# Two graph layers on one core: GpSimd sums Wh's rows for the mean, six blocks of adj come late, Wh runs seven blocks ahead

## The chip, the cores and the metric

The kernel runs on one core of a Trainium2 chip. The metric is the device time of one execution in microseconds; lower is better. Each core has five engines with instruction queues of their own: TensorE (PE in the profile; its weight loads are PEld), VectorE (DVE), ScalarE (ACT), GpSimd (POOL) and SyncE (SP, which here only issues DMAs). DMAs are also issued from the queues of ACT and GpSimd.

## What is computed

x is 4096 x 512 in float32. adj is 4096 x 4096 in int32, with about four ones in a row. Two layers follow one another:

```
Wh   = einsum(x, W)                        # 8 heads of 64
f1, f2 = Wh . a[:, :64], Wh . a[:, 64:]    # a number per node and head
e    = leaky_relu(f1[:, None] + f2[None, :], 0.2), and -9e15 where adj is 0
x1   = layernorm(x + softmax(e) @ Wh)

agg  = (mask @ x1) / max(deg, 1)
out  = layernorm(x1 + relu(concat(x1 @ W_self + b_self, agg @ W_nb + b_nb) @ W_comb + b_comb))
```

A row of adj without a single one gives a softmax over equal values: the node gets the mean of all rows of Wh. That mean is what a part of this change is about.

## The kernel before

The nodes are cut into 32 blocks of 128 (P). The kernel turns each row of adj into a list of its neighbours, and then gathers rows by index from tables in DRAM, with no dense product over adj. The order of the instructions of each engine is the order in which the program text issues them (`manual_schedule`); each engine works through its own in that order, with semaphores between engines.

**First stage** (the loop at L979, `for b in range(LB)`). For each block b of adj, SP loads two halves of 1 MB (`load_adj`, buffers `at`, four of them), two blocks ahead. ACT turns a half into bfloat16 and counts it (`mask_adj`, L448, three `ab` buffers). TensorE folds a block's masks into keys (`fold_adj`, L467), and VectorE takes the eight largest of each quarter (`max_keys`, L482). Every fourth block, `decode` turns four blocks' keys into neighbour lists, indices (`idx`) and owner masks (`own`). It is a generator with 16 stops; `some(lists)` runs it from stop to stop, in this loop four times a step. Near its end it builds four step tiles on VectorE (`place(b)`, L545 and L546), which TensorE multiplies (L551).

Beside that, Wh is computed block by block (w). `transposed` turns x's block on TensorE and ACT copies it out as xT; `node_half` multiplies xT with the weights, 264 columns at a time (L376), and VectorE copies the result to `row` (L380). GpSimd copies three small parts (`node_rest`) and stores the row to table t0 (`store`, L976). There are 32 node blocks and 27 loop steps, so the steps in AHEAD = (1, 6, 11, 16, 20) do two node blocks. The last row is stored by SP, after the loop (L1010).

For the mean, `transposed` also sums x over the nodes: for most blocks with four ACT copies that carry a sum (L368), for four of them with a reduction on VectorE (L365), and for the last three with additional transposes (`only=True`). `mean_row` then multiplies the mean of x by the weights at steps 23 to 26 and stores it as row 1 of t0. Row 0 of t0 is a pad whose scores are very negative; node n is in row n + 2.

**Late blocks.** Blocks LB + 1 to 31 of adj (28 to 31) are not loaded in this loop. After it, `load_late` brings quarters of 0.5 MB, and `mask_late` (L967, ACT) masks them; the dictionary MASKS says how many at each step of the attention loop. A block whose four quarters are in is folded and maximised at the next step (`full`).

**The crossing** (L1010 to L1058). SP stores the last row, loads two late quarters and the weights w_nb and w_comb, which TensorE multiplies together (`fold_weights`, L302 and L314; `place` takes `row` buffers). GpSimd gathers the first blocks from t0, five rows for each node (`gather`, L641: k = 0 is the node's first neighbour, k = 1 to 4 are shared slots). Blocks LB - 1 and LB are folded here. The decode of blocks 24 to 27 starts here (L1033), with its step tiles in a `row` buffer (`on_row`), and runs on at the first attention steps.

**The attention loop** (L1066, i from -3). A step works on several blocks at once: a_shared(i+1) on TensorE (L715), gathers for block i+6 once a buffer is free, a_weights and a_weigh on VectorE (L672, L690), a_first (L698) on VectorE and a_own_sum (L708) on ACT, the layer norm on ACT, the transposition (L355) and a_z (L759). At i == TURN (8) the lists of blocks 28 to 31 begin to be decoded, and w_self is loaded into m1, which up to then holds the late quarters. The third stage does the second layer in the same manner, from table t1.

Of the kernel before, what the change touches and what calls it, by code (L numbers as in the profile page):

```python
# [40 lines left out]
P = 128  # L41
# [72 lines left out]
def listed_layers(  # L114
# [33 lines left out]
    AHEAD = (1, 6, 11, 16, 20)  # L148
    EARLY = NB - 3
    LB = NB - 5  # L150
    FIRST = (0, 1, 3, *range(LB + 1, NB))

    t0 = tc.dram_tile([N + 2, FW], F32, name="t0")
    t1 = tc.dram_tile([N + 2, HD], F32, name="t1")
# [120 lines left out]
    def pads(wp):  # L275
        pad = wp.tile([P, FW], F32, name="row", bufs=3)
        nc.vector.memset(pad[0:1, 0:H], -BIG)
        nc.vector.memset(pad[0:1, H:FW], 0.0)
        nc.scalar.dma_start(t0[0:1, :], pad[0:1, :])
        nc.scalar.dma_start(t1[0:1, :], pad[0:1, H:TW])  # L280
        nc.scalar.dma_start(t1[1:2, :], pad[0:1, H:TW])
# [67 lines left out]
    def transposed(b, wp, sums=None, only=False):  # L349

        tp = ps.tile(
            [P, FB, P], F32, name="pw" if only else "tp", bufs=2 if only else 1
        )
        for c in range(FB):
            nc.tensor.transpose(tp[:, c, :], xs[:, b, ts(c, P)], ident)  # L355
        if only:
            t = tp
        else:
            t = wp.tile([P, FB, P], F32, name="xT", bufs=4)
        if sums is None or b >= EARLY and not only:  # L360
            nc.scalar.copy(t, tp)
        elif only or b % 2 == 0 and b < XL:
            if not only:
                nc.scalar.copy(t, tp)
            nc.vector.tensor_reduce(sums[:, :, b : b + 1], tp, AX.X, OP.add)  # L365
        else:
            for c in range(FB):
                nc.scalar.activation(  # L368
                    t[:, c, :], tp[:, c, :], AF.Copy, accum_out=sums[:, c, b : b + 1]
                )  # L370
        return t
# [10 lines left out]
    def node_first(b, xT, w_sb, row, between):  # L382
# [5 lines left out]
        for n, (k, r) in enumerate(parts):  # L388
# [6 lines left out]
            if n == 2:  # L395
                fold_adj(between, dp)
                max_keys(between)
            if n > 1:
# [9 lines left out]
    def mean_row(w_sb, sums, xa):  # L408

        xm = small.tile([P, FB], F32, name="xm", bufs=1)  # L410
        nc.vector.tensor_reduce(xm, sums, AX.X, OP.add)
        nc.vector.tensor_scalar(xm, xm, 1.0 / N, None, OP.mult)
        yield
        mr = xa.tile([1, FW], F32, name="mr")
        mf = small.tile([1, H], F32, name="mf", bufs=1)
        for k in range(2):
            pq = ps.tile([1, HW], F32, name="sm", bufs=2)
            for c in range(FB):
                nc.tensor.matmul(
                    pq, lhsT=xm[:, c : c + 1], rhs=w_sb[:, c, k * HW : (k + 1) * HW],  # L420
                    start=(c == 0), stop=(c == FB - 1),
                )
            nc.vector.tensor_copy(
                mr[0:1, k * HH : (k + 1) * HH], pq[:, (1 - k) * H : (1 - k) * H + HH]
            )
            if k == 0:
                nc.vector.tensor_copy(mf, pq[:, 0:H])
                yield
        nc.gpsimd.dma_start(t0[1:2, 0:H], mf)
        nc.gpsimd.dma_start(t0[1:2, TW:FW], mf)  # L430
        nc.gpsimd.dma_start(t0[1:2, H:TW], mr[0:1, 0:HD])
        yield
# [51 lines left out]
    def decode(b0, dp, place):  # L484
# [36 lines left out]
        nc.vector.tensor_scalar(L[:, :, 0:1], L[:, :, 0:1], 1.0, None, OP.max)  # L521
        nc.vector.tensor_scalar(idx[:, bs, 0:K0], L[:, :, 0:K0], float(N + 1), None, OP.min)
# [127 lines left out]
    def gather(table, b, g, at=None):  # L650
        for k in range(KS) if table is t0 else (*range(1, KS), 0):
# [970 lines left out]
```

## Time and profile before

| | us |
|---|---|
| median of three runs | 659.75 (653.55 to 661.48) |
| the profiled execution's own time | 768.31 |
| its span, first to last instruction | 766.6 |
| busy: PE, DVE, ACT, POOL | 596.7, 410.3, 408.9, 356.4 |
| last `row` copy of the first stage ends | 201.3 |
| first gather from t0 starts | 204.33 |

All times in what follows are of that one profiled execution, measured from its first instruction. In lists of groups, a line reads: source line, engine, operation, output <- inputs, shapes, how many | busy time and mean ns of one | idle time of the engine before them and what ended it. In timelines, a line has the start, the length, the engine, the line, the operation, and in brackets how long the engine stood idle before and who released it. "remote" and "issue" mean that the profile names no releaser. An x of 8 for matmuls stands for four float32 matmuls, recorded as two passes each.

### The profile page before, as it was taken

What the parts mean: (1) busy time and instruction counts of PE and PEld (TensorE: products, weight loads), DVE (VectorE), ACT (ScalarE), POOL (GpSimd) and SP (SyncE); (2) the same over time, 40 slices, a digit from 0 to 9 for tenths busy, and PEclk for the clock granted to TensorE, in tenths of its full rate; (3) what the DMA queues carried; (4) which work ended last, traced back from release to release, by engine and by line L of the source; (5) the groups of instructions that cost most, each with busy time, mean ns of one, the idle gap of its engine ahead of it and who ended that gap; (6) DMA issues with size and microseconds to landing.
All of it is one profiled execution on the core that took longest, in us unless ns stands there. A gap on an engine that the chain in (4) does not pass through costs nothing.

```text
span 766.6 us, 9427 instructions
## 1 busy us (share of the span) xinstructions
PE 596.7 (78%) x2582; PEld 296.2 (39%) x2582; DVE 410.3 (54%) x1186; ACT 408.9 (53%) x1066; POOL 356.4 (46%) x475
## 2 busy tenths in 40 slices
PE   6798898989763677797596678875956997877794
PEld 4576576766431232343242333332312332222231
DVE  6265869768773566566666655564212423333243
ACT  3588887887511376664454446453324434443355
POOL 4112111221475355654565544465566666666630
PEclk9799999999867798988898898998988899999998
DMA  8999999999795599886876756677678787777762
GB/s 267 408 407 409 408 409 407 410 386 389 267 327 145 166 309 323 302 270 215 255 210 209 241 175 201 222 225 240 232 215 269 238 273 254 242 248 242 256 223 86
DMA packets 92197, 210.44 MB, mean 275 GB/s; under 512 B 13854, under 2 KB 13862, under 8 KB 92138
## 3 DMA queue, kind: packets, MB, share of 16 engines
q1 hardware_dynamic: 63296, 114.32, 40.5%
q0 software_dynamic: 28656, 95.18, 39.8%
q8 instruction: 23, 0.38, 0.2%
q10 hardware_dynamic: 186, 0.28, 0.2%
q14 instruction: 36, 0.29, 0.1%
HBM read 175.91 MB, written 33.82 MB: 274 GB/s over the span
## 4 chain that ended last, share of the span: by engine, by line
PE 36%; issue 15%; DMA 14%; DVE 11%; another core or an unknown queue 11%; ACT 11%; SPq 1%; POOL 0%; DVEq 0%; ACTq 0%; POOLq 0%
DMA at<-in_adj_dram 12%; PE pw L759 6%; PE pw L376 6%; PE pw L785 5%; PE nm L785 5%; PE num L715 4%; ACT ab L448 3%; PE pw L314 3%; PE nm L792 2%; PE pw L792 2%; DVE g L690 1%; DVE sm L808 1%; PE tp L355 1%; DVE num L728 1%
## 5 line engine op out<-in xcount | busy, mean ns | idle before, releaser
L641 POOL DMA_INDIRECT g<-t,idx x290 | 276.3, 953 | 193.0 <-issue 85.5
L759 PE MATMUL pw<-wr,xT 128*128 128x512 f32 x256 | 130.1, 655 | 8.1 <-issue 8.1
L376 PE MATMUL pw<-w_sb,xT 128*128 128x264 f32 x496 | 125.8, 400 | 2.9 <-DVE row L380 1.4
L448 ACT ACTIVATE ab<-at 128x2048 bf16<-128x2048 int32 x56 | 107.1, 1916 | 33.2 <-DMA at<-in_adj_dram 27.0
L376 PEld LDWEIGHTS pw<-w_sb,xT 128*128 128x128 f32 x496 | 91.9, 194 | 28.1 <-issue 3.4
L715 PE MATMUL num<-g,own 128*32 128x256 f32 (+1 forms) x512 | 40.6, 441 | 54.7 <-ACT num L708 50.0
L759 PEld LDWEIGHTS pw<-wr,xT 128*128 128x128 f32 x256 | 50.8, 209 | 75.9 <-issue 73.5
L402 POOL COPY lst<-row 128x8 f32<-128x8 f32 x32 | 6.9, 216 | 151.9 <-DVE row L380 121.7
L690 DVE TENSOR_TENSOR g<-g,ew 128x2048 f32<-128x2048 f32 x32 | 73.1, 2283 | 2.1 <-ACT xs L754 1.3
L785 PE MATMUL nm<-m,xT 128*128 128x512 f32 x128 | 62.5, 627 | 6.8 <-issue 5.4
L785 PE MATMUL pw<-m,xT 128*128 128x512 f32 x128 | 64.5, 643 | 3.6 <-issue 2.0
L723 DVE RECIPROCAL rd<-num 128x8 f32<-128x8 f32 x32 | 6.6, 208 | 104.6 <-PE num L715 46.9
L808 DVE SCALAR_TENSOR_TENSOR sm<-g,lst,nm 128x512 f32<-128x512 f32 x15 | 11.3, 754 | 82.5 <-remote 45.1
L355 PE MATMUL tp<-ident,xs 128*128 128x128 f32 x256 | 41.5, 287 | 14.0 <-ACT xT L368 6.8
L776 ACT COPY nm<-brow 128x512 f32<-128x512 f32 x16 | 9.4, 585 | 76.5 <-DVE sm L808 45.2
L355 PEld LDWEIGHTS tp<-ident,xs 128*128 128x128 f32 x256 | 31.9, 147 | 38.0 <-issue 24.2
L680 ACT ACTIVATE ew<-e 128x40 f32<-128x40 f32 x32 | 6.6, 206 | 74.8 <-issue 35.5
L380 DVE COPY row<-pw 128x264 f32<-128x264 f32 x62 | 26.4, 426 | 31.9 <-PE pw L376 24.5
L763 ACT COPY row<-pw 128x512 f32<-128x512 f32 x32 | 18.7, 584 | 46.0 <-remote 23.6
L715 PEld LDWEIGHTS num<-g,own 128*32 128x32 f32 x512 | 14.5, 119 | 73.4 <-ACT num L708 56.5
L785 PEld LDWEIGHTS pw<-m,xT 128*128 128x128 f32 x128 | 25.3, 205 | 43.8 <-issue 39.0
L785 PEld LDWEIGHTS nm<-m,xT 128*128 128x128 f32 x128 | 24.1, 197 | 44.5 <-issue 38.2
(240 smaller groups left out, 967.1 us busy)
## 6 DMA issues: line engine op xcount, KB each, us to landing
at<-in_adj_dram SPq DMA_DIRECT2D x56, 1024.0 KB
m<-in_adj_dram SPq DMA_DIRECT2D x16, 512.0 KB
xt<-xT SPq DMA_DIRECT2D x32, 256.0 KB
t<-row SPq DMA_DIRECT2D x32, 256.0 KB
xT<-xt SPq DMA_DIRECT2D x32, 256.0 KB
out_dram<-row SPq DMA_DIRECT2D x32, 256.0 KB
t<-row POOLq DMA_DIRECT2D x31, 264.0 KB
xs<-in_x_dram SPq DMA_DIRECT2D x31, 256.0 KB
```

The lines of the kernel that those rows point to most:

```text
L314: nc.tensor.matmul(mp, lhsT=wT[:, d, :], rhs=wc[:, d, :], start=(d == 0), stop=(d == FB - 1))
L355: nc.tensor.transpose(tp[:, c, :], xs[:, b, ts(c, P)], ident)
L376: nc.tensor.matmul(pw, lhsT=xT[:, c, :], rhs=w_sb[:, c, k * HW : (k + 1) * HW], start=(c == 0), stop=(c == FB - 1),)
L380: nc.vector.tensor_copy(row[:, k * HW : (k + 1) * HW], pw)
L448: nc.scalar.activation(ab, loads.pop((b, h)), AF.Relu, accum_out=asum[:, b, h : h + 1])
L641: nc.gpsimd.indirect_dma_start(out=out, out_offset=None, in_=table, in_offset=bass.IndirectOffsetOnAxis(ap=at, axis=0),)
L690: nc.vector.tensor_tensor(gv, gv, E[b][:, sl].unsqueeze(3).to_broadcast([P, sl.stop - sl.start, H, D]), OP.mult,)
L715: nc.tensor.matmul(NM[b][ts(k, HP), a * HD : a * HD + r.stop - r.start], lhsT=OWN[b][:, k, :], rhs=G0[b][:, K0 + k, r], start=False, stop= ...
L759: nc.tensor.matmul(pz, lhsT=xT[:, c, :], rhs=m2[:, c, :], start=(c == 0), stop=(c == FB - 1))
L785: nc.tensor.matmul(NM[b], lhsT=xT[:, c, :], rhs=m1[:, c, :], start=False, stop=(c == FB - 1), skip_group_check=True,)
L792: nc.tensor.matmul(NM[b][ts(k, HP), :], lhsT=OWN[b][:, k, :], rhs=g[:, K0 + k, 0:HD], start=False, stop=True, tile_position=(0, k * HP), s ...
L808: nc.vector.scalar_tensor_tensor(yp, Y[b], lst[:, b, KL + 1 : KL + 2], NM[b], OP.mult, OP.add)
```

## The change

1. LB goes from 27 to 25: blocks 26 to 31 of adj come late, six instead of four, and the loop has 25 steps. AHEAD becomes seven steps, (0, 3, 6, 9, 12, 16, 20).
2. The sums over x are gone. GpSimd adds each row of Wh, but the last, into `acc` (`add_row`), after the row's store. `mean_row` multiplies `acc` and the last row by a column of 1/4096 on TensorE, and SP stores the result as row N + 2 of t0. It stands after the last row's store and after block 24's fold, ahead of the late loads.
3. Row 1 of t0 becomes a second pad. In `decode`, a node without neighbours gets index N + 2 for k = 0. In `gather`, the own row (k = 0) comes last for both tables, and the others read a view of t0 without its last row.
4. In a doubled step, the second transposition and the second mask of the next block are issued between the two halves of the first node block (`then`).
5. The decode of blocks 24 to 27 no longer starts in the crossing. It starts in the attention loop, at the step where block 27's maxima are taken (i = 2), and its step tiles lie in an xT buffer. MASKS now runs to i = 11, so TURN is 12; w_self's fold moves from steps 10, 15, 20, 25 to 15, 19, 23, 27.

```diff
-    AHEAD = (1, 6, 11, 16, 20)
-    EARLY = NB - 3
-    LB = NB - 5
+    AHEAD = (0, 3, 6, 9, 12, 16, 20)
+    LB = NB - 7
...
-        nc.scalar.dma_start(t0[0:1, :], pad[0:1, :])
-        nc.scalar.dma_start(t1[0:1, :], pad[0:1, H:TW])
-        nc.scalar.dma_start(t1[1:2, :], pad[0:1, H:TW])
+        for r in range(2):
+            nc.scalar.dma_start(t0[r : r + 1, :], pad[0:1, :])
+            nc.scalar.dma_start(t1[r : r + 1, :], pad[0:1, H:TW])
+        nc.scalar.dma_start(t1[N + 2 : N + 3, :], pad[0:1, H:TW])
...
-        if sums is None or b >= EARLY and not only:
-            nc.scalar.copy(t, tp)
-        elif only or b % 2 == 0 and b < XL:
-            if not only:
-                nc.scalar.copy(t, tp)
-            nc.vector.tensor_reduce(sums[:, :, b : b + 1], tp, AX.X, OP.add)
-        else:
-            for c in range(FB):
-                nc.scalar.activation(
-                    t[:, c, :], tp[:, c, :], AF.Copy, accum_out=sums[:, c, b : b + 1]
-                )
+        t = wp.tile([P, FB, P], F32, name="xT", bufs=4)
+        nc.scalar.copy(t, tp)
...
+    def add_row(b, row):
+        if b == 0:
+            nc.gpsimd.tensor_copy(acc, row)
+        else:
+            nc.gpsimd.tensor_tensor(acc, acc, row, OP.add)
+
+    def mean_row(row, wp):
+
+        mr = wp.tile([P, FW], F32, name="row", bufs=3)
         for k in range(2):
+            r = slice(k * HW, (k + 1) * HW)
             pq = ps.tile([1, HW], F32, name="sm", bufs=2)
-            for c in range(FB):
-                nc.tensor.matmul(
-                    pq, lhsT=xm[:, c : c + 1], rhs=w_sb[:, c, k * HW : (k + 1) * HW],
-                    start=(c == 0), stop=(c == FB - 1),
-                )
...
-        nc.gpsimd.dma_start(t0[1:2, 0:H], mf)
-        nc.gpsimd.dma_start(t0[1:2, TW:FW], mf)
-        nc.gpsimd.dma_start(t0[1:2, H:TW], mr[0:1, 0:HD])
-        yield
+            for n, t in enumerate((acc, row)):
+                nc.tensor.matmul(pq, lhsT=inv_n, rhs=t[:, r], start=(n == 0), stop=(n == 1))
+            nc.vector.tensor_copy(mr[0:1, r], pq)
+        nc.sync.dma_start(t0[N + 2 : N + 3, :], mr[0:1, :])
...
-        nc.vector.tensor_scalar(L[:, :, 0:1], L[:, :, 0:1], 1.0, None, OP.max)
-        nc.vector.tensor_scalar(idx[:, bs, 0:K0], L[:, :, 0:K0], float(N + 1), None, OP.min)
+        ni = dp.tile([P, G, K0], F32, name="ni", bufs=1)
+        nc.vector.tensor_scalar(ni, L[:, :, 0:K0], 0.0, float(N + 2), OP.is_equal, OP.mult)
+        nc.vector.scalar_tensor_tensor(
+            idx[:, bs, 0:K0], L[:, :, 0:K0], float(N + 1), ni, OP.min, OP.max
+        )
...
-        for k in range(KS) if table is t0 else (*range(1, KS), 0):
+        for k in (*range(1, KS), 0):
             rows_of(
-                g[:, k, 0 : table.shape[1]], table, (idx if at is None else at)[:, b, k : k + 1]
+                g[:, k, 0 : table.shape[1]], table if k == 0 or at is not None else table[0 : N + 2, :],
+                (idx if at is None else at)[:, b, k : k + 1],
             )
...
         if not keep:
             store(w, row, nc.gpsimd)
+            add_row(w, row)
...
-    def on_row(b):
+    def on_xT(b):
         if b % G == 0:
-            steps_at[0] = wp.tile([P, FW], F32, name="row", bufs=3)
-        return steps_at[0][:, ts(b % G, P)]
+            steps_at[0] = wp.tile([P, FB, P], F32, name="xT", bufs=4)
+        return steps_at[0][:, b % G, :]
...
-        for k in range(1 + (b in AHEAD)):
-            nxt = transposed(w + 1, wp, sums) if w + 1 < NB else None
-            if k == 0 and 21 <= b < 24:
-                transposed(EARLY + b - 21, wp, sums, True)
-            if k == 0:
-                key_bank(b + 1)
-                for h in range(NH):
-                    mask_adj(b + 1, h)
-            row = node_block(w, xT, None if k or nxt is None else b, keep=nxt is None)
-            w, xT = w + 1, nxt
+        ahead = [transposed(w + 1, wp) if w + 1 < NB else None]
+        key_bank(b + 1)
+        mask_adj(b + 1, 0)
+
+        def then():
+            ahead.append(transposed(w + 2, wp))
+            mask_adj(b + 1, 1)
+
+        if b not in AHEAD:
+            mask_adj(b + 1, 1)
+        row = node_block(
+            w, xT, None if ahead[0] is None else b, keep=ahead[0] is None,
+            **(dict(then=then) if b in AHEAD else {}),
+        )
+        w, xT = w + 1, ahead[0]
+        if b in AHEAD:
+            node_block(w, xT)
+            w, xT = w + 1, ahead[1]
...
     store(w - 1, row, nc.sync)
+    fold_adj(LB - 1, dp)
+    max_keys(LB - 1)
+    mean_row(row, wp)
     for k in range(2):
         load_late()
...
-    fold_adj(LB - 1, dp)
-    max_keys(LB - 1)
...
-    lists = [decode(LB + 1 - G, dp, on_row)]
...
-    MASKS = {-1: 2, 0: 2, 1: 2, 2: 1, 3: 2, 4: 1, 5: 2, 6: 1, 7: 1}
+    MASKS = {-1: 2, 0: 2, 1: 2, 2: 2, 3: 2, 4: 1, 5: 2, 6: 1, 7: 2, 8: 2, 9: 1, 10: 2, 11: 1}
...
+        if NB - G - 1 in full:
+            lists = [decode(NB - 2 * G, dp, on_xT)]
...
-        if -3 < i < 1 or TURN < i <= TURN + 3:
+        if 0 < i <= TURN + 8:
             some(lists)
...
-        if i in (10, 15, 20, 25):
-            if i == 10:
+        if i in (15, 19, 23, 27):
+            if i == 15:
```

## The prediction

> **What bounds the kernel now.** The profiled execution took 768.31 us with a span of 766.6 us; the three plain runs have a median of 659.75 us (653.55 to 661.48). The profile is thus 108 us longer than what is measured. I work the sum out in its microseconds and carry the difference over to the median one for one, because the terms that matter (bytes at the DMA rate, TensorE instructions in the first stage) are busy time; the spans that the profile itself puts down to "issue" or an unknown queue (15% and 11% of its chain of waits) are where a profile would be long, and I take little from them.
>
> First view: the page's slices of the span (19.2 us each).
>
> ```profile
> PE   6798898989763677797596678875956997877794
> DMA  8999999999795599886876756677678787777762
> GB/s 267 408 407 409 408 409 407 410 386 389 267 327 145 166 309 323 302 270 215 255 210 209 241 175 201 222 225 240 232 215 269 238 273 254 242 248 242 256 223 86
> ```
>
> The reader should see a first stage of ten slices at 386 to 410 GB/s with a DMA share of nine tenths or more, and after it nothing that stays full. That stage is bound by bytes. Second view: the busy time of each engine in stretches of it.
>
> ```profile
> core 0: us, PE busy (x) PEld busy (x) DVE busy (x) ACT busy (x) POOL busy (x), PEclk, DMA share, GB/s
> 60.00:80.00 20.00, 16.91 (x99) 12.98 (x99) 11.74 (x42) 17.56 (x47) 3.28 (x12) 1.00 1.05 410
> 160.00:180.00 20.00, 17.57 (x106) 13.01 (x105) 13.71 (x54) 18.63 (x42) 4.61 (x16) 1.00 1.01 375
> 180.00:190.00 10.00, 9.22 (x52) 6.42 (x52) 8.22 (x30) 6.90 (x8) 0.92 (x4) 1.00 1.04 400
> 190.00:201.00 11.00, 11.00 (x61) 7.16 (x61) 8.05 (x38) 7.31 (x9) 3.81 (x11) 1.00 0.65 247
> ```
>
> TensorE is close behind the DMA (85 to 90%), ScalarE too; from 190 to 201 us the loads are done and TensorE alone, 11.00 of 11, finishes the last two node blocks. The stage ends when the last row of Wh is copied (200.87, L380) and stored by SP (201.33); the gathers start at 204.33. Third view: the timeline of what follows.
>
> ```profile
> 201.33 0.34 SPq L976 DMA_DIRECT2D t<-row  x1
> 201.72 0.97 SPq L952 DMA_DIRECT2D m<-in_adj_dram  x2
> ...
> 241.07 0.59 ACT L318 COPY wr<-pw 128x512 f32<-128x512 f32 x1 [13.50 <-remote]
> ...
> 257.29 0.89 DVE L482 MAX8 kk<-pw 128x8 f32<-128x128 f32 x4 [1.19 <-remote]
> 258.10 0.68 DVE L698 TENSOR_TENSOR num<-g,ew 128x512 f32<-128x512 f32 x1
> 258.68 0.28 DVE L545 TENSOR_SCALAR lt<-iota,end 128x128 f32<-128x128 f32 x1
> ...
> 259.42 0.76 PE L551 MATMUL tp<-lq,row 128*128 128x104 f32 x2 [6.63 <-DVE row L546]
> ```
>
> Two holes: one of 13.5 us that ends when the backlog of 25 gathers has drained (DMA falls to 8 GB/s at 240), and one of 6.63 us in which TensorE stands at a decode matmul (L551) for steps that VectorE makes late. After it, the attention steps follow one another by the starts of L690: 272.38 (block 4) to 324.15 (block 10) is 8.63 us a step, 324.15 to 505.04 (block 31) 8.61.
>
> **What the Trainium skill says.** "GPSIMD Engine Reference", section Elementwise — side-by-side cycle accounting, has an add of two float32 inputs of 2048 elements at 4497 ns on GpSimd; 520 elements would be 1.14 us by proportion. The trace has a two-input product, 1024 elements, at 2352 ns, so 1.19 us: they agree, and I use the trace. "SBUF — State Buffer", section Who interferes with whom, says that a VectorE instruction with two SBUF inputs contends with a GpSimd instruction that reads SBUF, and that the second to issue waits for the whole of the first. The trace is in line with it at most weakly: GpSimd's 8-element copies (L403) have a median of 185 ns and reach 630. The same page, section SBUF: two separate sides, has 432 GB/s measured for the DMA; here it fills at 407 to 410.
>
> ```profile
> L368 ACT ACTIVATE xT<-tp 128x128 f32<-128x128 f32 x100 | 26.1, 276 | 4.2 <-PE tp L355 4.2
> L368 ACT ACTIVATION_READ_ACCUMULATOR xT<-tp 128x1 f32 x100 | 20.8, 208 | 0.0
> L419 PE MATMUL sm<-w_sb,xm 128*1 128x264 f32 x16 | 3.9, 386 | 0.0
> L887 POOL TENSOR_TENSOR xs<-w_sb,xs 128x1024 f32<-128x1024 f32 x2 | 4.7, 2352 | 2.9 <-DMA w_sb<-in_L_gnn_W_dram 2.9
> ```
>
> **Part 1, two blocks fewer in the first stage.** Four loads of 1024 KB leave it: 4.19 MB at 408 GB/s is 10.3 us of the bounding resource. With them go four ACT masks (1.916 + 0.197 us each, 8.5), two key copies (1.2), two folds (0.62 each on PE). Those lie beside the DMA: nothing more.
>
> **Part 2, the mean.** Out: on ACT, 25 blocks of four copies with sums (46.9 us by the two rows above) become 25 plain copies of 0.588 (14.7): 32 us less. On VectorE, seven reductions (4.8 us). On PE, twelve transposes (1.8 us) and the mean's matmuls (3.9). All of it but the last is hidden behind the loads. The second half of the mean's matmuls starts at 195.13, where PE alone holds the end: 1.94 us off the path. In: 30 adds and a copy on GpSimd, 31 x 1.19 = 37 us, beside 36 us that it is busy in 181; its idle time before L402 (121.7 us) hides them, if the shared port doesn't. The tail's new matmuls, four of 264 columns, are about half of the old 3.9 us, with two row copies on VectorE of 0.43; they stand after the last row, and the mean's store stands on SP ahead of two late adj loads and two weight loads. PE needs the fold (0.62) and 1.9 us, then 0.4 for the copy: these four loads go some 3 to 4 us later against the last row. Behind them waits L967 on ACT, then L680, which today idles 10.43 us for VectorE; that hides it. On GpSimd, three DMA issues (1.6 us) go. Only the own-row gathers (k=0) read the mean; issued after four of 1.26 us each, they find it landed: nothing. Two more pad stores on ACT cost 0.26 each at step 4, under the load wait.
>
> **Part 3, seven doubled steps, reordered.** A single step moves 2.10 MB of adj, 0.26 of x and 0.27 of t0: 6.4 us at 408. PE's single step from 80.09 to 85.13 is 5.04. A doubled step adds about 4.4 us of PE (0.5 and twice 1.95) and 1.3 of DMA. Seven of them in 25 steps need 31 us, and the slack is 25 x 1.4 = 35: PE stays level with the DMA, just. x loads go on SP ahead of adj loads, same bytes. From below I allow 4 us of loss, from above 2 of gain (4 us of PE are idle from 20 to 35); I take 0. **Stage: -10.3 - 1.9 = -12.2**, between -7 (PE's own saving alone: 1.8 + 3.9 + 1.2) and -15.
>
> **Part 4, the decode of blocks 24 to 27 leaves the crossing.** In its place half of the decode of 20 to 23 runs there, about as much VectorE time (both some 8 to 10 us, by L510, L536, L546, L560). But no decode is left in the steps before block 27's keys are in, so the hole of 6.63 us at L551 goes. What is late next is a_first (L698, at 258.10) and ACT's L708; PE's fold of weights, which stood behind L551, can go first. I take -6.6; ends -8 and 0. The step tile moves from a row buffer to an xT buffer, of which two of four are in use: nothing. The gathers' backlog is the same 25 gathers after the last row, so the 13.5 us hole moves with the stage and stays: 0, ends -5 and +5.
>
> **Part 5, two blocks more late.** Eight half-loads (4.19 MB) where the DMA is at 203 to 280 GB/s; ACT 8 x 1.25 = 10 us, PE 2 x 2.5, VectorE 2 x 1.14, a decode of some 15 us of VectorE spread over eight steps. Steps with masks last 8.63 us today, those without 8.61; leaving the four longest out, (180.9 - 44.3)/17 = 8.03. So a mask step costs 0 to 0.6 us; four more, and decode in eight steps at a like price: 0 to +7. I take **+3**. The later fold of w_self has the same work and is used only in the next layer: 0.
>
> **Shared port:** I take +1, ends 0 and +37 (rival below). The rest of the edits (two decode lines swapped for two of about 0.2 us, gather order, buffers) have nothing that waits for them.
>
> **Sum:** -12.2 - 6.6 + 3 + 1 = -14.8, 768.3 to 753.5 in the profile, 659.75 to **645** at the median.
>
> **Rivals.** (A) The sum, chance 0.66; its own range 632 to 653.
> (B) **The waits come back**: PE, not bytes, ends the stage (-7), the hole at L551 is taken over by a_first (0), late blocks cost the whole 7: 660, chance 0.15. For it: PE at 11.00 of 11 in the tail. Against: PE idles 18 of 181 us in the stage, and the reorder feeds it earlier. That the mean holds the first gathers, so that the change doesn't do what it says, would be here too: the store is some 4 us behind the last row's, giving +4.
> (C) **GpSimd's adds hold VectorE at the shared port.** VectorE is at 125.6 of 181 us in the stage, and up to 18.2 of 20; its decode has many two-input steps, and the row copies (L380) that free PE's banks queue behind them. If every add costs its whole 1.19 us there, 37 - 14.8 = +22: 682. It cancels the gain from 0.48 us an add and passes 2% from 0.9. Against: the row copies and maxima have one input, from PSUM, and half the stage VectorE has room. Chance 0.19, with times from 673.
>
> **How the numbers follow.** Two per cent, 13.2 us, is about what a measurement of this kernel tells from no change: below 646.5 is faster, above 673 slower. Of A I put 0.55 below 646.5 (its upper terms come together: less for ACT, earlier PE work) and 0.11 above it. Of B 0.02, 0.11 and 0.02. C is slower. Together 0.57, 0.22, 0.21. The range is 628 to 672: it takes in A and B and leaves out C and the tip of A, about 0.2; A alone is 632 to 653.
>
> **What would show it.** Right: the last L380 near 189, DMA full until about 180; L448 52 times, L368's line gone for one copy of 0.59 per block; adds of about 1.2 us, VectorE's busy time in the stage not above 130; no decode matmul before block 3's L690; steps of 8.6 still in the middle. Wrong: VectorE's two-input steps stretched beyond 1 us beside adds, PE waiting for L380, the last row still after 195; first gathers waiting for the mean's store; mask steps of 9.5 us or more; a longer hole when the gathers drain.

## The result, and the profile after

The changed kernel takes 664.69 us (658.31 to 670.74), the kernel before 658.96 (653.55 to 662.35), 20 runs each: a ratio of 1.0086 with a 95% interval of 1.0057 to 1.0115. It is **slower by 0.9%**, by less than 2% and by more than its uncertainty. The sum said 645.

The executions fell on chips of two kinds: the kernel before takes about 658 us on the one and 759 to 767 on the other; the first profile of before (768.31) was of the second kind, and the result's runs and the profile after are of the first. Each chip was used for one group of runs only, so whether the difference lasts is not known. Ratios below always compare kernels on one chip. To read the two kernels side by side, I use a profile of the first kind in which the instructions of before are unchanged (`before_rows`, below).

The changed kernel's profiled execution took 662.42 us, with a span of 660.7. Its slices of the span (16.5 us each):

```profile
PE   7878999879993685886998999999799999999993
DMA  8999999998986979899899998898979999998883
GB/s 255 391 391 375 394 393 393 393 390 308 394 315 231 385 246 349 289 315 388 294 311 366 315 302 262 278 294 273 318 253 315 311 314 322 337 312 301 289 253 126
```

The first stage is still a plateau, but at 390 to 394 GB/s (one slice has 375) instead of 407 to 410, with the DMA just as full. Its end, in the busy time of each engine:

```profile
core 0: us, PE busy (x) PEld busy (x) DVE busy (x) ACT busy (x) POOL busy (x), PEclk, DMA share, GB/s
180.00:190.00 10.00, 10.00 (x66) 7.18 (x59) 9.55 (x37) 10.00 (x13) 4.99 (x11) 1.00 0.99 331
190.00:200.00 10.00, 8.34 (x45) 5.87 (x45) 9.48 (x30) 7.08 (x9) 3.32 (x8) 1.00 0.67 257
```

Two blocks fewer are loaded, yet PE is at 10.00 of 10 until 190 and VectorE at 9.5. The last row is copied at 199.7, where 189 was forecast. The groups on the page that answer to the forecast's rows:

```profile
L361 PE MATMUL pw<-w_sb,xT 128*128 128x264 f32 x496 | 126.6, 403 | 7.7 <-DVE row L365 7.7
L425 ACT ACTIVATE ab<-at 128x2048 bf16<-128x2048 int32 x52 | 99.3, 1910 | 38.4 <-DMA at<-in_adj_dram 36.0
...
L398 POOL TENSOR_TENSOR acc<-acc,row 128x528 f32<-128x528 f32 x30 | 39.5, 1318 | 0.6
```

The masks are 52, as forecast, and an add takes 1318 ns instead of 1.19 us (a row has 528 elements; the forecast took 520). What matters is the idle time of L361: PE waited 7.7 us for VectorE's row copies. The same group idles 2.9 us on the page of before:

```profile
L376 PE MATMUL pw<-w_sb,xT 128*128 128x264 f32 x496 | 125.8, 400 | 2.9 <-DVE row L380 1.4
```

The timeline of the crossing:

```profile
199.69 0.34 SPq L959 DMA_DIRECT2D t<-row  x1
202.95 0.31 SPq L409 DMA_DIRECT2D t<-row  x1
203.30 0.90 SPq L935 DMA_DIRECT2D m<-in_adj_dram  x2
...
204.76 0.60 SPq L286 DMA_DIRECT2D wc<-in_L_gnn_W_comb_dram  x1
...
223.35 0.75 DVE L333 SCALAR_TENSOR_TENSOR brow<-wc,bcol,brow 128x512 f32<-128x512 f32 x1 [7.16 <-DMA wc<-in_L_gnn_W_comb_dram]
223.46 5.38 PE L314 MATMUL pw<-wc,row 128*128 128x512 f32 x8 [5.40 <-DMA wc<-in_L_gnn_W_comb_dram]
224.37 2.28 DVE L671 TENSOR_TENSOR g<-g,ew 128x2048 f32<-128x2048 f32 x1
```

and in `before_rows`:

```profile
200.72 0.34 SPq L976 DMA_DIRECT2D t<-row  x1
202.64 0.51 SPq L286 DMA_DIRECT2D wc<-in_L_gnn_W_comb_dram  x1
217.78 0.74 DVE L333 SCALAR_TENSOR_TENSOR brow<-wc,bcol,brow 128x512 f32<-128x512 f32 x1
222.54 2.28 DVE L690 TENSOR_TENSOR g<-g,ew 128x2048 f32<-128x2048 f32 x1
```

The mean's store (L409) is issued 3.3 us after the row's; behind it stands w_comb's load, 5.1 us after the row's store where it was 1.9, and on VectorE a step (L333) waits 7.16 us for that load. The first weighing of the attention loop (L671, L690 before) comes right behind that step; before, the step waited for nothing and was done 4 us ahead.

Where the time went, from the starts of the weighing (a_weigh, L690 before, L671 after; block 0 to 31), first kind of chip:

| us | before_rows | after | difference | forecast |
|---|---|---|---|---|
| last row copy ends | 200.7 | 199.7 | -1.0 | -12.2 |
| to the weighing of block 0 | 21.8 | 24.7 | +2.9 | 0 |
| block 0 to 3 | 23.5 | 20.7 | -2.8 | -6.6 |
| block 3 to 13 | 73.0 | 84.7 | +11.7 | } |
| block 13 to 14 | 18.0 | 6.5 | -11.4 | } +3 |
| block 14 to 31 | 104.0 | 113.1 | +9.1 | } |
| rest | 211.0 | 211.2 | +0.2 | 0 |

The forecast's +1 for the shared port has no row here. The spans differ by 8.7 us (652.0 and 660.7), the medians of the result by 5.7: the profiled execution of `before_rows` is the fastest of its 22 (653.71, median 659.04), and the first kind has no other profile of before's instructions. For the changed kernel there are two more, `after_again` (666.3) and `after_aligned` (663.5), which take 115.9 and 117.1 us from block 14 to 31.

### The profile page after: what moved, and what is told of

The parts are those of the page before. It is cut to its first block, busy times and chain, and to the rows that moved or that the text cites. A ratio compares the mean times of both kernels' runs of the same rounds, so it can differ in the third digit from the quotient of the medians.

```text
span 660.7 us, 9277 instructions
## 1 busy us (share of the span) xinstructions
PE 572.1 (87%) x2569; PEld 288.1 (44%) x2570; DVE 423.6 (64%) x1176; ACT 396.5 (60%) x897; POOL 393.4 (60%) x503
## 4 chain that ended last, share of the span: by engine, by line
PE 45%; DMA 28%; DVE 12%; issue 6%; ACT 5%; POOL 2%; SPq 1%; POOLq 0%; DVEq 0%; ACTq 0%
DMA g<-t,idx 12%; PE pw L740 10%; PE pw L361 10%; DMA m<-in_adj_dram 7%; DMA at<-in_adj_dram 5%; PE nm L766 5%; PE pw L314 4%; PE pw L766 4%; DMA wc<-in_L_gnn_W_comb_dram 3%; PE num L696 2%; PE pw L773 2%; POOL g L621 2%; PE nm L773 2%; ACT abl L950 1%; DVE row L365 1%
## 5 line engine op out<-in xcount | busy, mean ns | idle before, releaser
L361 PE MATMUL pw<-w_sb,xT 128*128 128x264 f32 x496 | 126.6, 403 | 7.7 <-DVE row L365 7.7
L740 PE MATMUL pw<-wr,xT 128*128 128x512 f32 x256 | 122.2, 621 | 0.7 <-ACT xT L355 0.7
L425 ACT ACTIVATE ab<-at 128x2048 bf16<-128x2048 int32 x52 | 99.3, 1910 | 38.4 <-DMA at<-in_adj_dram 36.0
L361 PEld LDWEIGHTS pw<-w_sb,xT 128*128 128x128 f32 x496 | 93.4, 197 | 32.3 <-DVE row L365 10.8
L671 DVE TENSOR_TENSOR g<-g,ew 128x2048 f32<-128x2048 f32 x32 | 73.0, 2283 | 6.9 <-ACT ew L661 6.9
L740 PEld LDWEIGHTS pw<-wr,xT 128*128 128x128 f32 x256 | 47.8, 197 | 61.0 <-issue 60.1
L766 PE MATMUL pw<-m,xT 128*128 128x512 f32 x128 | 58.8, 602 | 0.0
L355 ACT COPY xT<-tp 128x512 f32<-128x512 f32 x64 | 37.2, 582 | 22.8 <-PE tp L353 19.3
L365 DVE COPY row<-pw 128x264 f32<-128x264 f32 x62 | 26.3, 425 | 34.4 <-PE pw L361 27.2
L696 PE MATMUL num<-g,own 128*32 128x256 f32 (+1 forms) x512 | 35.6, 396 | 11.7 <-ACT num L689 11.7
L398 POOL TENSOR_TENSOR acc<-acc,row 128x528 f32<-128x528 f32 x30 | 39.5, 1318 | 0.6
L766 PEld LDWEIGHTS pw<-m,xT 128*128 128x128 f32 x128 | 23.4, 190 | 35.2 <-issue 29.1
L789 DVE SCALAR_TENSOR_TENSOR sm<-g,lst,pw 128x512 f32<-128x512 f32 x15 | 11.3, 756 | 41.2 <-PE pw L773 37.9
L621 POOL DMA_INDIRECT g<-t,idxe x30 | 28.7, 957 | 10.5 <-issue 5.2
```

Of the source, the lines that this page charges most:

```text
L361: nc.tensor.matmul(pw, lhsT=xT[:, c, :], rhs=w_sb[:, c, k * HW : (k + 1) * HW], start=(c == 0), stop=(c == FB - 1),)
L365: nc.vector.tensor_copy(row[:, k * HW : (k + 1) * HW], pw)
L398: nc.gpsimd.tensor_tensor(acc, acc, row, OP.add)
L425: nc.scalar.activation(ab, loads.pop((b, h)), AF.Relu, accum_out=asum[:, b, h : h + 1])
L621: nc.gpsimd.indirect_dma_start(out=out, out_offset=None, in_=table, in_offset=bass.IndirectOffsetOnAxis(ap=at, axis=0),)
L671: nc.vector.tensor_tensor(gv, gv, E[b][:, sl].unsqueeze(3).to_broadcast([P, sl.stop - sl.start, H, D]), OP.mult,)
```

## The experiments

**First four: which part of the mean costs what.** All on one chip of the second kind. `no_adds` is after without the adds (the store and the matmuls of the mean stay):

```
-        else:
-            nc.gpsimd.tensor_tensor(acc, acc, row, OP.add)
```

> The changed kernel without the 30 adds on GpSimd (acc holds block 0's row alone, so the mean row is left out in effect). Theory port: the adds hold VectorE's one-input steps in the first stage for up to 1.3 us each, and with them gone the stage ends 4 to 10 us earlier, ratio to the kernel before 0.993 to 1.002. Theory late loads: the loss is in the attention loop's four more mask steps (about 2 us each), the adds cost nothing at the end, ratio 1.006 to 1.011 as with them.

`old_mean` is after with the mean of before (ACT's sums, VectorE's reductions, the extra transposes, the matmuls at steps 21 to 24, stored from GpSimd's queue as row N + 2); `add_row` is gone:

```
-            add_row(w, row)
-    mean_row(row, wp)
+        if b == 21:
+            pieces = mean_row(w_sb, sums, xa)
+        if b >= 21:
+            next(pieces, None)
```

> The changed kernel, but the mean made as before from sums of x on ACT and VectorE, with its extra transposes at steps 19 to 21. Theory port: better than the changed kernel by 3 to 8 us, ratio to before 0.995 to 1.003. Theory late loads: no better, 1.006 to 1.015.

`adds_only` is before with the new mean (adds, table rows, gather order and index), and LB, AHEAD, the decode's place and MASKS as they were:

```
+            add_row(w, row)
...
+    fold_adj(LB - 1, dp)
+    max_keys(LB - 1)
+    mean_row(row, wp)
```

> The kernel before (four late blocks, five doubled steps, decode of 24 to 27 in the crossing), with only the mean taken over: adds on GpSimd, mean as the table's last row. Theory port: slower than before, 1.005 to 1.02, as VectorE is held and ACT, which was not the bound, gains nothing. Theory late loads: not slower, 0.99 to 1.002, since ACT and PE lose work.

> The kernel before, unchanged, for a second profile: its first profiled execution took 768 us where plain runs take 659. If late loads bound the mask steps in it too, its attention steps with masks (i -1 to 7) take about 8.4 us and those without about 6.4, as in the changed kernel; if a step costs the same with masks and without (my prediction), both are near 6.5 to 7. If the adds on GpSimd are what spoils the first stage, VectorE's busy time up to 200 us is again near 126 us here (the changed kernel: 146) and the last row copy ends at 195 to 201.

`before_again` took 764.53 (one run, beside a median of 759.16 for before on this chip). The ratios to before: `no_adds` 0.9881 (0.9851 to 0.9911), `old_mean` 0.9926 (0.9899 to 0.9954), `adds_only` 1.0225 (1.015 to 1.03). The last row copy ends at 192.0, 199.8 and 207.3 us, against 200.4 in `before_again` and 199.7 in after. So the adds cost the stage 7.6 us, and the old mean costs it as much; `after` is of the other kind of chip here, but the stage of before ends alike on both (200.4 and 200.7). The ratios of `no_adds` and `old_mean` lie below the ranges expected for them, that of `adds_only` just above. VectorE's busy time from 20 to 200 us is 132.5 in after, 125.2 in `before_again` and 122.8 in `no_adds`; the 146 of the expectation is not that stretch's. VectorE's groups between 20 and 200 us, in after:

```profile
L525 DVE TENSOR_SCALAR lt<-iota,end 128x128 f32<-128x128 f32 x20 | 12.0, 601 | 0.5
...
L492 DVE TENSOR_SCALAR va<-nb 128x64 f32<-128x64 f32 x5 | 7.8, 1552 | 0.2
...
L471 DVE TENSOR_TENSOR kk<-kk,top 128x128 f32<-128x128 f32 x12 | 5.0, 414 | 0.4
```

The first two in `before`:

```profile
L545 DVE TENSOR_SCALAR lt<-iota,end 128x128 f32<-128x128 f32 x20 | 5.7, 284 | 0.5
L515 DVE TENSOR_SCALAR va<-nb 128x64 f32<-128x64 f32 x6 | 1.2, 195 | 0.2
```

and in `no_adds`, whose lines are three lower:

```profile
L522 DVE TENSOR_SCALAR lt<-iota,end 128x128 f32<-128x128 f32 x20 | 5.7, 284 | 0.5
L489 DVE TENSOR_SCALAR va<-nb 128x64 f32<-128x64 f32 x6 | 1.2, 206 | 0.2
```

A step of 64 elements grows from 195 to 1552 ns with the adds, and is back without them. After's timeline shows one of them:

```profile
183.33 0.56 POOL L959 DMA_DIRECT2D t<-row  x1
183.74 1.55 DVE L492 TENSOR_SCALAR va<-nb 128x64 f32<-128x64 f32 x1
183.91 1.32 POOL L398 TENSOR_TENSOR acc<-acc,row 128x528 f32<-128x528 f32 x1
```

VectorE's step stands through the whole add and ends with it (185.3 and 185.2). All five steps of L492 do, and of the four steps of each decode at L525 one does (1.55 us; the other three take 0.28), which makes the mean of 601. L471, with two inputs from SBUF, grows from 293 to 414 ns in the mean, but eleven of its twelve steps meet no add; the one that does is held as well:

```profile
52.89 1.75 DVE L471 TENSOR_TENSOR kk<-kk,top 128x128 f32<-128x128 f32 x1
53.16 1.32 POOL L398 TENSOR_TENSOR acc<-acc,row 128x528 f32<-128x528 f32 x1
```

The nine row copies (L365, input from PSUM) that overlap an add take 432 to 434 ns, and none of the 62 takes more. I count 18 held steps, together 18 us longer than the same steps in `no_adds`. Behind them queue the row copies that free PE's banks. PE's wait for them falls with the adds; in the groups of `no_adds`, between 20 and 200 us:

```profile
L361 PE MATMUL pw<-w_sb,xT 128*128 128x264 f32 x496 | 124.0, 399 | 0.6 <-DVE row L365 0.6
```

That is 0.6 us where after has 7.7. GpSimd also keeps the `row` buffers longer with the adds, but VectorE's row copies wait for it only 3.2 us in after and 1.2 in `no_adds`. In `old_mean` the same matmuls wait 8.0 us, 4.1 of them for VectorE's reductions:

```profile
L377 PE MATMUL pw<-w_sb,xT 128*128 128x264 f32 x496 | 126.6, 404 | 8.0 <-DVE sums L366 4.1 <-DVE row L401 2.0 <-DVE row L381 2.0
```

The old mean also gives TensorE its transposes and matmuls back; how its 7.8 us divide between the waits and that work, no run tells.

**What slowed the loads.** `no_adds` and `old_mean` also run at 390 to 392 GB/s between 20 and 100 us, where `before_again` has 408, so the adds are not the reason. First theory: the tables, one row longer in DRAM. `before_rows` gives before the longer tables; `after_aligned` and `old_mean_aligned` put after's and `old_mean`'s at other offsets. On a chip of the first kind, with `after_again`:

```
-    t0 = tc.dram_tile([N + 2, FW], F32, name="t0")
+    t0 = tc.dram_tile([N + 3, FW], F32, name="t0")[0 : N + 2, :]
```

> The kernel before with its two tables allocated one row longer (N + 3) and no other change: same instructions, other addresses. Theory address: the four kernels with N + 3 rows so far move 391 to 394 GB/s in the first stage (2 KB packets of 88 ns in the mean), the two with N + 2 408 (84 ns); this one moves 392, its last row copy ends at 204 to 208 instead of 200 to 201, ratio 1.004 to 1.012. Theory order: the rate comes from the changed instruction order or the missing sums; this one moves 408, ratio 0.998 to 1.002.

> The changed kernel unchanged, beside the runs of this call, since times differ from chip to chip. Ratio to the kernel before 1.003 to 1.012, as in the result, on any chip; if the late loads are what costs, less on a chip where gathers are slower and steps long anyway.

```
-    t0 = tc.dram_tile([N + 3, FW], F32, name="t0")
+    t0 = tc.dram_tile([N + 66, FW], F32, name="t0")[0 : N + 3, :]
```

> The changed kernel with the tables allocated N + 66 and N + 4 rows long (both a multiple of 4096 bytes longer than in the kernel before), of which it uses the same N + 3. Theory address: 406 to 409 GB/s in the first stage, better than the changed kernel beside it by 3 to 8 us. Otherwise no difference (within 2 us).

> The changed kernel with the mean from sums of x (no adds on GpSimd) and with tables as in the run above. If adds and addresses each cost the first stage some 5 us, it is the best so far: 0.98 to 0.99 of the kernel before, last row copy at 190 to 194. If only one of them does, 0.988 to 0.995.

The theory fell: `before_rows` stays at 408 GB/s (ratio 1.0018, 0.9999 to 1.0037), `after_aligned` at 390 (1.0084, 1.0048 to 1.0121). `after_again` repeats the result (1.0128, 1.0091 to 1.0165). `old_mean_aligned` has 0.9985 (0.9964 to 1.0005): with the old mean the rest of the change gains nothing measurable on this chip, where 0.98 to 0.995 was expected, and it is the new mean that makes it slower. The traces of `old_mean_aligned` and `after_aligned` say where. The last row copy ends at 199.1 and 199.4; the first weighing comes 22.3 and 27.1 us later, that of block 3 another 17.9 and 21.1; from there to block 31 both take 206. So new for old costs nothing in the stage and 8 us in the crossing (6.3 between the medians), where the mean's matmuls and store stand ahead of SP's loads. The other profiles agree: the first weighing comes 24.7 to 27.1 us after the last row copy in all eleven with the new mean, `no_adds` and `adds_only` among them, and 21.8 to 22.5 in all nine with the old.

Second theory: the addresses in SBUF. The new tile `ni` of 16 bytes a partition shifts what is laid out behind it: the `at` buffers start on multiples of 512 bytes in before (143872 and so on), and 480 past one in after (143840), as the two programs lay them out. The buffers of the masks and the decode move with them, those that x is loaded into do not. I padded `ni`, first to 64 bytes (`at` then 448 past):

```
-        ni = dp.tile([P, G, K0], F32, name="ni", bufs=1)
+        ni = dp.tile([P, G, 4], F32, name="ni", bufs=1)[:, :, 0:K0]
```

> The changed kernel with its new small tile ni given 64 bytes a partition instead of 16. Nothing else differs but SBUF addresses: the at buffers, which adj is loaded into, start at multiples of 64 bytes again, as in the kernel before (in the changed kernel they start 32 bytes past one). Theory SBUF address: the first stage moves 405 to 409 GB/s, 2 KB packets take 84 ns in the mean, the last row copy ends at 194 to 198, ratio to before 1.000 to 1.008. If the rate has another cause: 392 GB/s, 88 ns, ratio as the changed kernel's (1.009 to 1.013).

> The changed kernel with the mean from sums of x on ACT and VectorE and with ni of 64 bytes. Both theories of the first stage (address, adds) together: last row copy at 190 to 194, then the crossing as with the old mean (some 40 us to the fourth weighing) and a loop that is still about 10 us longer by late loads: ratio 0.988 to 0.996.

> The changed kernel without the 30 adds and with ni of 64 bytes (the mean row is left out in effect). Last row copy at 186 to 190, VectorE busy 120 to 128 us up to 200, ratio 0.983 to 0.992. Against after_ni64 it gives the price of the adds alone: theory port says 5 to 8 us; if the adds are hidden, under 2.

A miss: 391 to 393 GB/s in all. Ratios (second kind): 0.9949 (0.9894 to 1.0003), 0.9964 (0.9925 to 1.0003), 0.9893 (0.9658 to 1.0128). The last row copies, 197.5 with the adds (197.0 in `dry_late_ni64` below, whose first stage is the same) and 191.2 without, repeat the cost of the adds: about 6 us. The ratios don't, as the interval of `no_adds_ni64` is wider than the difference.

Then both ways: `before_shift` puts the 16-byte tile into before, and the three `ni512` kernels bring `at` back to multiples of 512.

```
+        ni = dp.tile([P, G, K0], F32, name="ni", bufs=1)
+        nc.vector.memset(ni, 0.0)
```

> The kernel before with one more small tile (16 bytes a partition, set to zero once in each decode) in the pool that lies ahead of the adj buffers: they start 32 bytes below a multiple of 512 bytes, as in the changed kernel, instead of on one. Theory SBUF address: the first stage moves 391 to 394 GB/s, 2 KB packets take 88 ns in the mean, last row copy at 204 to 208, ratio 1.004 to 1.012. Else: 408 GB/s and 0.998 to 1.002.

```
-        ni = dp.tile([P, G, K0], F32, name="ni", bufs=1)
+        ni = dp.tile([P, G, 32], F32, name="ni", bufs=1)[:, :, 0:K0]
```

> The changed kernel with ni of 512 bytes a partition: the adj buffers start at multiples of 512 bytes, as in the kernel before (with 64 bytes they started at 448 past one, and the rate stayed at 392). Theory SBUF address, with the boundary at 512: 405 to 409 GB/s where adj streams, last row copy at 192 to 197, and 2 to 7 us less than the changed kernel. Else 392 GB/s and no difference.

> As above with the mean from sums of x, no adds on GpSimd. Last row copy at 188 to 195 if the rate comes back; ratio to before 0.985 to 0.995, the best of all if adds and address each cost. If the rate is not what ends the stage here (TensorE is), it stays at 199 and 0.996 to 0.999.

The same stretch of the first stage, columns as above; `before_again`, `before_shift` and `after_ni512` in this order:

```profile
20.00:100.00 80.00, 70.72 (x379) 51.08 (x378) 44.81 (x172) 62.95 (x140) 15.46 (x56) 0.94 1.05 408
```

```profile
20.00:100.00 80.00, 65.51 (x363) 46.82 (x362) 45.03 (x172) 60.71 (x138) 14.54 (x52) 0.98 1.05 392
```

```profile
20.00:100.00 80.00, 73.31 (x411) 54.67 (x411) 49.30 (x166) 56.33 (x69) 35.69 (x75) 0.98 1.05 404
```

Sixteen bytes make 392 of 408 at a full DMA, and PE gets 65.5 us of work done instead of 70.7. `before_shift` copies the last row at 208.0 (+7.6) and has 1.011 (1.0036 to 1.0185). `adds_only` has the shift too, and its 207.3 is as late from the shift alone: in the old order, the new mean in place of the old moves the end of the stage by nothing that shows. In the crossing it loses more: the first weighing comes 26.7 us after the last row copy, 22.0 in `before_shift`. Restoring the address gives 196.4 in `after_ni512`, 3.3 us less than in after. The size is rough: the two dry kernels below with the same first stage end it at 197.7 and 193.8, the five profiles with adds and shifted buffers in the new order at 197.0 to 199.7. The ratios: `after_ni512` 0.9925 (0.9882 to 0.9968), `old_mean_ni512` 0.9869 (0.9793 to 0.9945), whose last row is copied at 194.9.

**Are the late blocks' bytes the cost in the attention loop?** `dry_late` leaves out the loads of eight late quarters; the masks then read what is in the buffer:

```
+            if 2 <= n < 10:
+                return
```

> after_ni64 without 8 of the 24 late half-megabyte loads (the third to the tenth; the masks, folds and maxima of those quarters run on the data left in the buffer, so blocks 26 to 28 get other blocks' neighbours). Theory late loads: the attention loop waits for these loads, two at a time, about 10 us to land each, and becomes 8 to 14 us shorter, ratio 0.985 to 0.995. Theory engines: it is the masks' work on ACT and the decode on VectorE that lengthens the steps, and it stays within 3 us of after_ni64.

> after_ni512 without 8 of the 24 late half-megabyte loads (the third to the tenth; their quarters are masked from data already in the buffer, so blocks 26 to 28 get other blocks' neighbours). On a chip where the kernel before takes 658: the attention loop from the fourth to the last weighing is 6 to 14 us shorter than after_ni512's if its mask steps wait for loads, within 3 us if engines bound them. On a chip where it takes 760: within 4 us, as steps are long there for the gathers.

> The kernel of dry_late_ni512 once more (8 of the 24 late loads left out, their quarters masked from data in the buffer), for a chip on which the kernel before takes 658. There the changed kernel's loop takes 204 to 207 us from the fourth to the last weighing and the kernel before's 195. Theory late loads: 191 to 199 here. Theory engines: 203 to 207.

> The kernel of old_mean_ni512 once more, for the same kind of chip: its loop stays at 204 to 207 us (the late loads are all there), its last row copy at 193 to 196, ratio to before 0.988 to 0.998.

Ratios: 0.9965 (0.9908 to 1.0023), 1.0029 (0.9982 to 1.0077), 0.9857 (0.9771 to 0.9943); the last two are one kernel, so these two chips differ by more than the intervals. All fell on chips of the second kind. There, from the weighing of block 3 to that of 31, `after_ni512` takes 240.8 us and the dry kernel 242.1 and 246.2: with fewer bytes nothing is gained that shows, though one kernel differs by more than that between two chips (236.3 in `old_mean_ni512`, 245.8 in its repeat). These runs don't answer for the first kind, where the same stretch takes 195.0 us in `before_rows` and 204.4 in after. `old_mean_again`, `old_mean_ni512` once more, has 0.985 (0.9786 to 0.9915).

The loop on the first kind is read from its traces alone. Block 3 to 14, then 14 to 31, in `before_rows` and then in after:

```profile
246.00:337.00 91.00, 73.21 (x372) 32.38 (x371) 60.28 (x122) 59.88 (x173) 53.71 (x57) 0.91 0.88 312
337.00:441.00 104.00, 98.73 (x513) 45.65 (x514) 88.37 (x168) 71.88 (x223) 76.13 (x81) 1.00 0.92 293
```

```profile
245.10:336.40 91.30, 71.94 (x369) 31.35 (x368) 68.30 (x157) 64.57 (x181) 50.96 (x55) 0.89 0.92 326
336.40:449.50 113.10, 105.10 (x545) 48.57 (x546) 94.67 (x192) 75.40 (x232) 80.93 (x85) 1.00 0.91 305
```

The later stretch is PE's in both: 98.73 of 104.00 and 105.10 of 113.10. What PE got to do there, in the groups of `before_rows` and of after for that stretch:

```profile
L314 PE MATMUL pw<-wc,abl 128*128 128x512 f32 x24 | 10.9, 597 | 0.0
...
L302 PE MATMUL pw<-ident,m 128*128 128x128 f32 x8 | 1.2, 273 | 0.0
L551 PE MATMUL tp<-lq,last 128*128 128x104 f32 x8 | 1.1, 285 | 0.0
```

```profile
L314 PE MATMUL pw<-wc,abl 128*128 128x512 f32 x32 | 14.7, 601 | 1.0 <-ACT row L744 0.6 <-ACT abl L303 0.4
...
L302 PE MATMUL pw<-ident,m 128*128 128x128 f32 x16 | 2.5, 276 | 0.9 <-ACT row L744 0.9
L531 PE MATMUL tp<-lq,last 128*128 128x104 f32 x8 | 1.1, 285 | 0.0
L444 PE MATMUL pw<-abl,fold 128*32 128x512 bf16 x4 | 1.0, 380 | 0.1
L444 PE MATMUL pw<-last,fold 128*32 128x512 bf16 x4 | 0.8, 384 | 0.0
L444 PE MATMUL pw<-cols,two 128*32 128x512 bf16 x4 | 0.4, 379 | 0.0
```

What is new there is one more part of w_self's fold (3.8 + 1.3 us, with 1.9 of idle time) and the last late block's keys (2.2); the decode's matmuls (L551, L531) are the same. Groups overlap in part: PE's busy time grew by 6.4 us and its idle time by 2.7, together the 9.1.

The stretch that this work left, block 3 to 14, is as long as before, from two changes that cancel. In `before_rows` the first part of w_self's fold stands in the step from block 13 to 14. TensorE waits there 2.8 us for w_self's load and 3.7 for w_comb's, VectorE waits for TensorE, and the step takes 18.0 us:

```profile
332.81 0.21 DVE L723 RECIPROCAL rd<-num 128x8 f32<-128x8 f32 x1 [11.47 <-PE num L715]
```

In after that step takes 6.5. But the ten steps before it, in which 17 late masks lie instead of 12, and besides them the decode of blocks 24 to 27, take 84.7 us instead of 73.0. Masks of the late blocks end more waits there; after's waits between 238 and 337 us (total, times, longest):

```profile
POOL g L621 <- ACT last L950: 20.4, 5, 8.3
...
PE pw L444 <- ACT abl L950: 11.0, 6, 3.1
...
ACT abl L950 <- DMA m<-in_adj_dram: 8.5, 5, 2.3
```

In `before_rows` the same rows are 2.5, 4.3 and 2.6. No run put w_self's fold back to its old steps alone, nor the decode, so this account is read from the traces, not shown by an edit, and the 11.7 us are not divided between masks, keys and decode. The best versions run, `old_mean_ni512` and its repeat, are 1.3 and 1.5% faster than before on chips of the second kind; they were not run on the first, where the nearest, `old_mean_aligned` with the shifted buffers, equals before. The changed kernel with its tile padded is not slower on the second kind either (0.9949 and 0.9925).

## Why the prediction was wrong

**Part 1, two blocks fewer (-10.3), and Part 3, the reorder (0).** Right as sums, as far as the runs show, and taken away by others. `no_adds` still has the mean's matmuls after the last row and copies that row at 192.0, 8.7 us before `before_rows`; with some 3 us more for the address (196.4 in `after_ni512` against 199.7) that is about -12, where -12.2 was forecast. This adds up runs of different chips; the two edits weren't run together with aligned buffers. Without the adds TensorE kept level: in `no_adds` the DMA is full until 190 us, and the last row is copied 2 us later.

**Part 2, "its idle time before L402 hides them, if the shared port doesn't".** The port didn't, and this is the step that failed in the stage. The add's size was near (1318 ns for 1.19 us); its cost was entered as +1 and is 6 to 7.6 us. It was rival C in kind, and its sign came: the one two-input step of L471 that met an add took 1750 ns. But most of the time went to steps that C had left out, the float32 tensor_scalar with one input, from SBUF, which grew eightfold. The Trainium skill, "SBUF — State Buffer", section Who interferes with whom, has both halves: tensor_scalar can enter a mode that takes both port pairs, and then "Whoever issues first gets the shared pair for the whole instruction; the other **fully blocks**". I had used its rule for two inputs alone. The trace agrees on the blocking (1552 ns for 195, beside an add of 1318), but not on who is first: L492 is recorded 0.17 us ahead of the add and is held all the same. In which mode the step ran, and who had the ports, no run shows. Against C the prediction said that the row copies have one input from PSUM: true, they are not stretched, but they queue behind the steps that are. (C's 682 counts the +1 for the port twice; it should have been 681.)

**Part 2, the removals.** "All of it but the last is hidden behind the loads" failed too, in the other direction: in the new order the old mean costs as much (199.8 against 192.0 in `no_adds`), where 1.9 us was forecast for its removal. TensorE waits 4.1 us for VectorE's reductions there, 1.4 before. Hence new for old gained nothing in the stage, and lost in the crossing.

**Part 2, the tail: "that hides it".** The late loads do go later by what was forecast (3 to 4 us; 3.2 from the row's store). What waits isn't ACT at L680 but VectorE at L333 and PE at L314, for w_comb. I counted SP's queue and named one waiter; the other two loads behind it had their own. To the first weighing it costs 2.9 us in after and 4.7 in `after_again`, and the kernels with the old mean do not pay it (22.1 to 22.5 us to the first weighing).

**The load rate of 408, taken over for the changed kernel,** is a step without a line of its own: no term for a tile of 16 bytes. It costs before 7.6 us when put in alone, and after some 3. There PE, busy for 10.00 of 10 us until 190, ends the stage as much as bytes do, which is what rival B had named.

**Part 4, the hole at L551 (-6.6).** The mechanism was right: no decode matmul stands in the crossing, and the stretch is 2.8 us shorter. The size came from a profile of the other kind of chip; in `before_rows` PE waits 2.3 us for L546 there, not 6.63:

```profile
PE tp L551 <- DVE row L546: 2.3, 1, 2.3
```

**Part 5 (+3, ends 0 and +7).** Measured +9.4, outside its range. "A mask step costs 0 to 0.6 us" came from an execution in which all steps take 8.6 us, so masks looked free in it; here the ten steps with the added late work grew by 11.7 us, where all of the part was allowed 7. "The later fold of w_self has the same work ... : 0" failed too, in both directions: the step that its first part left became 11.4 us shorter, and the stretch that got it, where PE idles 5 of 104 us, 9.1 longer, 5 to 7 of it the fold's by the lines above.

**The range** of 628 to 672 held the time because it was wide, which is luck: stage, tail, hole and late blocks all came out dearer than their terms. The likeliest case did not come; B's 660 was nearest, with terms that I had spread over B and C.

## What to carry to other kernels

Before an operation is moved to GpSimd because that engine is idle, look at VectorE's float32 steps from SBUF to SBUF, with one input as with two, and at who queues behind them: the price is the wait of the next engine, not the busy time. A mean can hide it: ask for the single steps that ran beside the moved operation. Where a small tile is added, look at where the large DMA targets then start. Take the price of a step from an execution whose steps have the same pace as the one that will be measured, and look at moved work in its old place and its new one: equal work can hold up a step in the one and not in the other.

## What the runs showed of the hardware

- While loads of 1 MB streamed into buffers at multiples of 512 bytes (20 to 100 us), the DMA moved 404 to 408 GB/s, with buffers at 480 or 448 bytes past one 386 to 393, with its busy share full in both. The mean time of the 2 KB packets was 84.2 to 85.1 ns and 87.5 to 88.4. This holds for all 20 profiles, eight and twelve. Other offsets weren't tried, and why is open.
- A VectorE tensor_scalar of 128 x 64 in float32, SBUF to SBUF, that starts just ahead of a GpSimd add ends with it: 1552 ns for 195. A tensor_tensor of 128 x 128 with both inputs in SBUF did the same (1750 ns for 293); copies from PSUM beside an add kept their 432 to 434 ns.
- The same instructions of the attention loop, block 3 to 31, take 195.0 us on one chip and 240.1 on another (`before_rows` and `before_again`). Why is open; the first stage ends at 200.7 and 200.4.
